# Two bottleneck blocks on one core: the moments of one group of the 3x3 convolution a combination earlier, and smaller transfers at the very end

## The chip, the cores and the metric

The kernel runs on one core of a Trainium2 chip. The metric is device time in microseconds (us) of one execution, from the median of several. TensorE (PE) multiplies matrices, VectorE (DVE), ScalarE (ACT) and GpSimd (POOL) work on elements, and SyncE (SP) issues most of the transfers between the chip's memory (SBUF) and device memory.

## The reference

Two residual bottleneck blocks follow each other, each on 64 images of 1024 channels and 14x14 points, all in float32:

```python
out = relu(bn(conv(x, w1, b1, 1, 0), g1, be1))      # 1x1, 1024 -> 256 channels
out = relu(bn(conv(out, w2, b2, 1, 1), g2, be2))    # 3x3, 256 -> 256
out = bn(conv(out, w3, b3, 1, 0), g3, be3)          # 1x1, 256 -> 1024
x   = relu(x + softplus(residual_scale)[0] * out)
```

`bn` takes mean and variance of each channel over all 64 images and all points of this very batch. So no value can be normalised before its convolution is done for the whole batch, and each convolution ends with a point at which everything waits for the last statistics.

## The kernel before, in words

The activations between the convolutions (`y_all`, 128 partitions x 2 x 12544 float32) stay in SBUF. Images lie in pairs (`T` = 32 tiles of two) and, for the 3x3 convolution, in `NG` = 8 groups of `GI` = 8 images.

`conv2` (L549) is the 3x3 convolution, as a Winograd scheme over rows: each group is made of six combinations (`NF` = 6, three pairs in the order 1 and 2, 3 and 4, 5 and 0). For each combination, `combine` (L583) builds a sum of rows `r` on VectorE (L639 to L665), `sums` of its halves on VectorE (L596), `diffs` on GpSimd (L599), and loads the transformed filters on SP (L618). `Products` (L668) then multiplies on PE into PSUM banks `m`, `l`, `even` and `odd`. ScalarE copies `m` into `even` and `odd` as a start value (L697, L699) and copies `l` out into `ls` (L699). `finish` (L764) is a coroutine that takes the six combinations of a group one after the other and makes output rows out of them: in its tiles `a` (tag `fa`) and `d` (`fb`) it collects partial sums; rows 1 and 2 of every four are written at L795 and L796, row 3 and the end row at L810 and L811, and row 0 with the last combination `cb`. In the text a combination's place in its group is `k`, from 0 to 5.

Row 0 is `a` plus the columns of `cb`, where the columns are the PSUM bank plus or minus `ls`. In groups 0 to 6, VectorE writes bank and `ls` into `y` (L833, four instructions of 128x224) and two accumulating transfers on GpSimd's queue (L838) add `a` to it. In the last group (7) VectorE first adds `ls` into `a` (`cb.add`, L752, two instructions of 128x448) and then adds bank and `a` into `y` (L831), without a transfer.

The statistics of the 3x3 convolution come from two sources. For groups 0 to 6, and rows 1 and 2 of group 7, ScalarE passes over the rows with an accumulating activation (`moment`, L857: identity and square, for each of the two slots `o`), into the throw-away tile `idle`. For the rest of group 7 VectorE takes statistics (`stat`, L771, at L774). `merge` (L860) sums the moments up (a reduction on VectorE at L865 for each slot, the rest on GpSimd) into an entry beside those statistics. Then `aggregate` (L1168) and `affine` (L1184 to L1209) make scale and shift.

`long_work` (L890) says at which combination ScalarE does which long piece: the normalisation of the next group, or a moment of the group before. For the last group there is no next group, so its table differs. The order in which items go through the engines is the loop of L910 to L925; a scheduler then places the instructions on each engine where no order is written out, so that an edit may move neighbours.

After conv2 comes the Gram stage (`gram`, L935): the rows are normalised (ScalarE L539, VectorE L951), transposed (on PE at L981 for the first seven pieces, by transfers through `home` or `ws` and VectorE L993 for the rest) and multiplied with themselves on PE, which gives the statistics of the last convolution beforehand. Then the last convolution runs, in block 0 mixed with the first convolution of block 1.

In block 1 the last convolution is `final` (L1091): pairs of tiles, and at the end tile 31 alone with `residual` (L1074). It makes eight channel slots `o` one after the other: two matmuls, an addition with scale on VectorE (L1082), a ReLU on ScalarE (L1083); after every second slot SP issues a transfer of two slots to `out` (L1086).

Of the kernel before, what the change touches and what calls it, by code (L numbers as in the profile page):

```python
# [45 lines left out]
CS = C // P  # L46
MS = M // P
G = 2
T = N // G
# [16 lines left out]
NG = N // GI  # L66
# [25 lines left out]
def bottlenecks(ctx: ExitStack, tc: tile.TileContext, x, w1s, w2s, w3s, pars, out):  # L92
    nc = tc.nc
# [455 lines left out]
    def conv2(psum, pool, b, par, aff, affine_of, stats):  # L549
# [22 lines left out]
        def new(tag, tiles=RT):  # L572
            v = pool.tile([P, MS * RT * LINE], FP, tag=tag, name=tag, bufs=BUFS.get(tag, 1))
            return v[:, : MS * tiles * LINE].rearrange("p (s r l) -> p s r l", s=MS, r=tiles)
# [5 lines left out]
        def stt(to, a, by, c):  # L580
            return nc.vector.scalar_tensor_tensor(to, a, by, c, ALU.mult, ALU.add)
# [172 lines left out]
        def half(f, q):  # L754

            return f.rearrange("p o r (i q c) -> p q (o r i) c", i=GI, q=2)[:, q]

        def outputs(c):
            f = new("f", c.lines // GI)
            for q in c.banks:  # L760
                c.add(q, half(f, q), c.column(q))
            return f

        def finish():  # L764


            for g in range(NG):
                out_rows = [y_grp[:, :, g, k::4, :] for k in range(4)]
                last_group = g == NG - 1

                def stat(k, lines):  # L771
                    if last_group:
                        for o in range(MS):
                            nc.vector.bn_stats(stats[:, o, 1 + k, :], lines[o])  # L774

                ca = yield
                fa = None if ca.ls is None else outputs(ca)
                fb = outputs((yield))
                a, d = new("fa"), new("fb")
                if fa is not None:  # L780
                    nc.vector.tensor_add(a, fa, fb)
                    nc.vector.tensor_sub(d, fa, fb)
                else:
                    for q in ca.banks:
                        nc.vector.tensor_tensor(half(a, q), ca.column(q), half(fb, q), ALU.add)
                        nc.vector.tensor_tensor(half(d, q), ca.column(q), half(fb, q), ALU.subtract)

                fa = outputs((yield))
                fb = outputs((yield))
                c, e = new("fc", full), fa  # L790
                nc.vector.tensor_add(c, fa, fb)
                nc.vector.tensor_sub(e, fa, fb)
                a3, d3 = (v[:, :, :full] for v in (a, d))
                for o in range(MS):
                    stt(out_rows[1][:, o, :full], e[:, o], 2.0, d3[:, o])  # L795
                    stt(out_rows[2][:, o], c[:, o], 4.0, a3[:, o])  # L796
                nc.vector.tensor_add(a3, a3, c)
                stt(d3, e, 8.0, d3)
                if g == 0:
                    begin(out_rows[1][:, :, :full])  # L800
                if last_group:
                    for o in range(MS):
                        lines = y_grp[:, o, g, 1 : 1 + 4 * full].rearrange("p (r k) l -> p r k l", k=4)[:, :, :2]
                        for k in range(2):
                            moment(lines, idle[:, : 2 * full * LINE].rearrange("p (r k l) -> p r k l", k=2, l=LINE), o, k, g)

                fa = outputs((yield))

                end = y_grp[:, :, g, H - 1]
                nc.vector.tensor_add(out_rows[3], d3, fa[:, :, :full])  # L810
                nc.vector.tensor_add(end, d[:, :, full], fa[:, :, full])  # L811
                stat(0, [out_rows[3][:, o] for o in range(MS)])
                stat(1, [end[:, o] for o in range(MS)])
                if last_group:
                    merge()

                cb = yield
                if last_group:
                    for q in cb.banks:
                        cb.add(q, half(a, q), half(a, q))  # L820

                for j, q in enumerate(cb.banks):
                    for o in range(MS):
                        to, more = (
                            v[:, o].rearrange("p r (i q c) -> p q r i c", i=GI, q=2)[:, q] for v in (out_rows[0], a)
                        )
                        bank, ls = (
                            v[:, o].rearrange("p (r i c) -> p r i c", r=RT, c=WH) for v in (cb.banks[q], cb.ls)
                        )
                        if last_group:  # L830
                            nc.vector.tensor_add(to, bank, more)  # L831
                        else:
                            nc.vector.tensor_tensor(to, bank, ls, ALU.add if q == EVEN else cb.op)  # L833
                    stat(2 + j, [out_rows[0][:, o].rearrange("p r (i q c) -> p q r i c", i=GI, q=2)[:, q] for o in range(MS)])
                if not last_group:

                    for o in range(MS):
                        nc.gpsimd.dma_start(out=out_rows[0][:, o], in_=a[:, o], accum_op=ALU.add)  # L838
            yield
# [8 lines left out]
        def begin(lines):  # L848

            mv = small.tile([P, MS, nc.vector.BN_AGGR_DIM], FP, tag="mv_first", name="mv_first")  # L850
            for o in range(MS):
                nc.vector.bn_stats(first_stats[:, o], lines[:, o])
            for o in range(MS):
                nc.vector.bn_aggr(mv[:, o, :], first_stats[:, o])
            nc.vector.tensor_scalar(center, mv[:, :, 0], -1.0, None, ALU.mult)

        def moment(y, to, o, k, g):  # L857
            act(to, y, (AF.Identity, AF.Square)[k], bias=center[:, o : o + 1], accum_out=moments[:, o, k, g : g + 1])

        def merge():  # L860

            n = GPX * (NG - 1) + 2 * full * LINE
            m = small.tile([P, MS, 2], FP, tag="m12", name="m12")
            for o in range(MS):
                nc.vector.tensor_reduce(m[:, o], moments[:, o], mybir.AxisListType.X, ALU.add)  # L865
            eng = nc.gpsimd
            eng.tensor_scalar(m, m, 1.0 / n, None, ALU.mult)
            var = small.tile([P, MS], FP, tag="m12var", name="m12var")
            eng.tensor_tensor(var, m[:, :, 0], m[:, :, 0], ALU.mult)
            eng.tensor_sub(var, m[:, :, 1], var)  # L870
            eng.tensor_sub(m[:, :, 0], m[:, :, 0], center)

            for half in range(2):
                to = stats[:, :, 0, 3 * half : 3 * half + 3]
                eng.memset(to[:, :, 0], n / 2)
                eng.tensor_copy(to[:, :, 1], m[:, :, 0])
                eng.tensor_scalar(to[:, :, 2], var, n / 2, None, ALU.mult)
# [12 lines left out]
        def long_work(g, k):  # L890

            i = ("norm 0", "norm 1", 0, 1, 2, 3)[k] if g else (None, "norm 0", "norm 1", None, None, None)[k]
            if g + 1 == NG:
                i = (None, 0, 1, 2, 3, None)[k]
            if i in ("norm 0", "norm 1"):
                s = int(i[-1])
                norm(s, y_grp[:, s, g + 1], aff, act)
            elif i is not None:  # L900
                o = i // 2
                moment(y_all[:, o, (g - 1) * GPX : g * GPX], idle, o, i % 2, g - 1)

        made, finished = items(), finish()
        next(finished)
        queue = [next(made) for i in range(3)]
        queue[0].start()
        for k in range(NG * NF):  # L910
# [14 lines left out]
            queue = queue[1:] + list(itertools.islice(made, 1))  # L925
# [148 lines left out]
    def residual(psum, xt, b, t, w3, aff, made=()):  # L1074

        scale, shift = aff
        to = mids[t] if b == 0 else out[t]
        step = 2 if b == 1 and t == T - 1 else CS
        for o in range(CS):
            ps = made[o] if o < len(made) else conv3(psum, t, o, w3)  # L1080
            v = xt[:, o, :]
            nc.vector.scalar_tensor_tensor(v, ps, scale[:, o : o + 1], v, ALU.mult, ALU.add)  # L1082
            nc.scalar.activation(v, v, AF.Relu, bias=shift[:, o : o + 1])  # L1083
            if (o + 1) % step == 0:
                queue = nc.gpsimd if step == CS else nc.sync
                queue.dma_start(  # L1086
                    out=to[:, (o + 1 - step) * PX : (o + 1) * PX],
                    in_=xt[:, o + 1 - step : o + 1, :].rearrange("p s f -> p (s f)"),
                )
# [294 lines left out]
```

## Time and profile before

| | |
|---|---|
| median of 4 runs | 1990.44 us (1990.05 to 1991.28) |
| the profiled execution: its time, its span | 1992.06 us, 1990.3 us |
| granted PE clock, mean | 0.991 of full speed |
| first conv2: last matmul ends, first of the Gram stage starts | 597.14 us, 603.32 us |
| second conv2: the same | 1581.66 us, 1587.83 us |
| last matmul of all ends | 1985.34 us |

The profile is of one execution with its start at 0. A line of a timeline gives start in us, duration in us, engine, source line, operation, output `<-` inputs with their shapes, a count, and in brackets how long the engine had been idle and what released it. Rows that follow each other without a break on one engine overlap by some 0.08 us, since the next starts while the last drains. A line of windows gives a stretch, its length, each engine's busy time in it with the number of instructions, then the granted PE clock, the busy share of the DMA engines and GB/s.

### The profile page before, as it was taken

Reading aid. Unit: us, or ns where it says so; the run is one execution under the profiler, and the core shown is the slowest. Engines: PE = TensorE matmul, PEld = TensorE weight load, DVE = VectorE, ACT = ScalarE, POOL = GpSimd, SP = SyncE. Lnnn points to the kernel's source line nnn. Section 1 sums busy time; section 2 is a strip of 40 time slices with the busy share of each in tenths; the row PEclk is TensorE's granted clock in tenths of the full one; section 3 lists DMA queues with packets and bytes.
Section 4 is the critical chain, followed back from the end, with each engine's and each line's share of the span. In section 5 each row is a group of like instructions: output and inputs, shape, how many; then the busy total and the mean of one; then the engine's idle time right before and its main releaser. Section 6 shows DMA issues by size and latency. Waiting matters only on the chain.

```text
span 1990.3 us, 27740 instructions
## 1 busy us (share of the span) xinstructions
PE 1943.4 (98%) x9560; PEld 1638.4 (82%) x9560; DVE 1572.6 (79%) x2844; ACT 955.5 (48%) x1947; POOL 690.7 (35%) x738
## 2 busy tenths in 40 slices
PE   9999999999998999999999999999999899999998
PEld 5555558999997889999999999989999887555554
DVE  5788758999888567776776777699999874899997
ACT  2222214556565055555555555445556541555555
POOL 0111101333325133333333333223242260766665
PEclk9999999999999999999999999999999998999999
DMA  7876725676757534444444444266777485699998
GB/s 276 291 252 244 256 97 183 171 208 202 203 157 203 192 130 163 188 169 170 186 163 174 183 162 182 85 202 192 210 197 207 131 206 203 242 340 333 342 335 293
DMA packets 191341, 414.09 MB, mean 208 GB/s; under 512 B 27296, under 2 KB 159040, under 8 KB 174688
## 3 DMA queue, kind: packets, MB, share of 16 engines
q1 hardware_dynamic: 161728, 329.06, 48.3%
q0 software_dynamic: 24000, 32.39, 7.1%
q10 hardware_dynamic: 5472, 50.86, 6.1%
q8 instruction: 76, 1.25, 0.3%
q14 instruction: 65, 0.53, 0.1%
HBM read 267.95 MB, written 115.87 MB: 193 GB/s over the span
## 4 chain that ended last, share of the span: by engine, by line
PE 80%; DVE 13%; DMA 4%; ACT 2%; issue 1%; POOL 0%; DVEq 0%; SPq 0%; ACTq 0%
PE ay L172 17%; PE cy L172 13%; PE cp L172 11%; PE ap L172 10%; PE even L172 6%; PE odd L172 6%; PE ax L172 5%; PE m L172 5%; PE l L172 4%; PE cx L172 4%; DMA x<-mid 2%; DVE x L456 2%; DMA out<-x 1%; PE ps L172 1%; DVE sums L596 1%
## 5 line engine op out<-in xcount | busy, mean ns | idle before, releaser
L330 ACT ACTIVATE cu<-cy,scale 128x196 f32<-128x196 f32 (+1 forms) x552 | 256.8, 474 | 297.6 <-PE cy L172 290.3
L599 POOL TENSOR_TENSOR diffs<-r 128x448 f32<-128x448 f32 (+1 forms) x80 | 139.1, 1756 | 328.5 <-DVE r L643 150.0
L330 ACT ACTIVATE x<-x,shift 128x392 f32<-128x392 f32 x368 | 211.7, 614 | 68.8 <-POOL x L482 52.8
L456 DVE SCALAR_TENSOR_TENSOR x<-cp,scale,x 128x196 f32<-128x196 f32 (+1 forms) x368 | 178.1, 484 | 83.0 <-PE cp L172 81.0
L477 POOL TENSOR_TENSOR x<-x,cu 128x196 f32<-128x196 f32 (+1 forms) x184 | 167.5, 910 | 170.9 <-ACT cu L330 170.5
L172 PE MATMUL cy<-ct,ws 128*128 128x196 f32 (+1 forms) x736 | 221.7, 383 | 2.5 <-ACT cu L330 2.5
L172 PE MATMUL ay<-at,ws 128*128 128x196 f32 (+1 forms) x752 | 209.3, 381 | 1.0 <-ACT au L330 1.0
L482 POOL TENSOR_TENSOR x<-x,cu 128x392 f32<-128x392 f32 x124 | 125.9, 1015 | 190.7 <-DVE x L456 185.9
L172 PEld LDWEIGHTS ay<-at,ws 128*128 128x128 f32 x752 | 136.3, 190 | 35.1 <-ACT au L330 1.9
L172 PEld LDWEIGHTS cy<-ct,ws 128*128 128x128 f32 x736 | 133.6, 190 | 36.9 <-ACT cu L330 3.8
L503 POOL TENSOR_TENSOR x<-x,cu 128x392 f32<-128x392 f32 x120 | 125.0, 1042 | 83.6 <-DVE x L456 75.7
L172 PE MATMUL m<-sums,ua 128*128 128x224 f32 (+1 forms) x752 | 145.5, 336 | 0.0
L172 PEld LDWEIGHTS m<-sums,ua 128*128 128x128 f32 x752 | 131.4, 189 | 0.2
L456 DVE SCALAR_TENSOR_TENSOR x<-cx,scale,x 128x196 f32<-128x196 f32 (+1 forms) x184 | 89.2, 485 | 50.8 <-PE cx L172 50.5
L172 PE MATMUL cy<-y,w 128*128 128x196 f32 (+1 forms) x404 | 126.6, 400 | 0.0
L172 PE MATMUL even<-v,ub 128*128 128x224 f32 (+1 forms) x640 | 123.8, 334 | 1.6 <-ACT even L699 1.6
L172 PE MATMUL cx<-y,w 128*128 128x196 f32 (+1 forms) x404 | 125.3, 396 | 0.0
L172 PE MATMUL odd<-v,ub 128*128 128x224 f32 (+1 forms) x640 | 123.8, 335 | 0.1
L172 PE MATMUL l<-diffs,ub 128*128 128x224 f32 (+1 forms) x640 | 122.0, 333 | 0.0
L172 PE MATMUL cp<-zt 128*128 128x257 f32 x392 | 119.8, 387 | 1.9 <-DVE zt L987 1.7
L330 ACT ACTIVATE au<-ay 128x196 f32<-128x196 f32 (+1 forms) x141 | 53.6, 380 | 140.3 <-PE ay L172 139.6
L172 PE MATMUL cp<-y,ws 128*128 128x196 f32 (+1 forms) x368 | 113.7, 391 | 3.7 <-DVE x L456 2.3
(217 smaller groups left out, 4392.3 us busy)
## 6 DMA issues: line engine op xcount, KB each, us to landing
x<-in_x SPq DMA_DIRECT2D x62, 1568.0 KB, 6.8
ub<-u SPq DMA_DIRECT2D x80, 768.0 KB, 4.8
x<-mid SPq DMA_DIRECT2D x32, 1568.0 KB, 10.2
mid<-x ACTq DMA_DIRECT2D x31, 1568.0 KB, 5.1
out<-x SPq DMA_DIRECT2D x124, 392.0 KB, 7.0
ua<-u SPq DMA_DIRECT2D x94, 256.0 KB, 3.0
ub<-u SPq DMA_DIRECT2D x14, 1024.0 KB, 5.9
u<-y POOLq DMA_DIRECT2D x40, 256.0 KB, 6.3
```

The lines of the kernel that those rows point to most:

```text
L172: tc.keep_in_program_order(nc.tensor.matmul(*args, **kw))
L330: tc.keep_in_program_order(nc.scalar.activation(*args, **kw))
L456: nc.vector.scalar_tensor_tensor(v, bank, self.scale[:, o : o + 1], v, ALU.mult, ALU.add)
L477: nc.gpsimd.tensor_add(self.part(1, 1), self.part(1, 1), u3)
L482: nc.gpsimd.tensor_add(v, v, self.u12)
L503: nc.gpsimd.tensor_add(v, v, self.u12[:, i * self.n : (i + 1) * self.n])
L596: nc.vector.tensor_add(sums, r[:, :, :, WH:], r[:, :, :, :WH])
L599: nc.gpsimd.tensor_sub(diffs, r[:, :, :, :WH], r[:, :, :, WH:])
```

## The change

In `finish`, group 6 is completed the way the last group was: `ls` is added into `a`, then bank and `a` into `y`, both on VectorE; the two accumulating transfers of that group go. In `long_work`, the four moments of group 6 move from `k` = 1 to 4 of the last group to `k` = 0 to 3. In `residual`, the last tile of all goes out in five transfers in place of four: slots 0 and 1, 2 and 3, 4 and 5, then 6 alone, all on SP, then 7 alone on ScalarE's queue.

```diff
@@ finish
+                by_transfer = g < NG - 2
...
                 cb = yield
-                if last_group:
+                if not by_transfer:
                     for q in cb.banks:
                         cb.add(q, half(a, q), half(a, q))
...
-                        if last_group:
+                        if not by_transfer:
                             nc.vector.tensor_add(to, bank, more)
                         else:
                             nc.vector.tensor_tensor(to, bank, ls, ALU.add if q == EVEN else cb.op)
...
-                if not last_group:
+                if by_transfer:
 
                     for o in range(MS):
                         nc.gpsimd.dma_start(out=out_rows[0][:, o], in_=a[:, o], accum_op=ALU.add)
@@ long_work
             if g + 1 == NG:
-                i = (None, 0, 1, 2, 3, None)[k]
+                i = (0, 1, 2, 3, None, None)[k]
@@ residual
-        step = 2 if b == 1 and t == T - 1 else CS
+        tail = b == 1 and t == T - 1
         for o in range(CS):
...
+            step = CS if not tail else 1 if o + 2 >= CS else 2
             if (o + 1) % step == 0:
-                queue = nc.gpsimd if step == CS else nc.sync
+                queue = nc.gpsimd if step == CS else nc.scalar if o + 1 == CS else nc.sync
```

## The prediction

> **What bounds the kernel now.** I read the page first (shares, then the chain that ended last), then the timelines of the two places that the change touches, engine by engine, and at the end the windows with granted clock and DMA share.
>
> ```profile
> PE 1943.4 (98%) x9560; PEld 1638.4 (82%) x9560; DVE 1572.6 (79%) x2844; ACT 955.5 (48%) x1947; POOL 690.7 (35%) x738
> PE 80%; DVE 13%; DMA 4%; ACT 2%; issue 1%; POOL 0%; DVEq 0%; SPq 0%; ACTq 0%
> ```
>
> TensorE is busy 98% of the span and is 80% of the chain. So the change can only pay where PE stands still: at the end of each 3x3 convolution (conv2, one per block, PE idle 597.14 to 603.32 us and 1581.66 to 1587.83) and behind the last matmul (1985.34 to 1990.3). This is the end of the first conv2, in order of time (start, duration, engine, line):
>
> ```profile
> 594.09 0.19 ACT L330 ACTIVATION_READ_ACCUMULATOR idle<-y,center 128x1 f32 x1
> 594.30 1.60 ACT L330 ACTIVATE idle<-y,center 128x1568 bf16<-128x1568 f32 x1
> 594.35 1.26 DVE L774 BATCH_NORM_STATS2 stats<-y 128x6 f32<-128x336 f32 x4
> 595.45 1.69 PE L172 MATMUL odd<-v,ub 128*128 128x224 f32 x8
> 595.81 0.19 ACT L330 ACTIVATION_READ_ACCUMULATOR idle<-y,center 128x1 f32 x1
> 595.90 0.52 ACT L699 ACTIVATE ls<-l 128x448 f32<-128x448 f32 x1
> 596.03 0.17 DVE L865 TENSOR_REDUCE m<-moments 128x2 f32<-128x16 f32 x1 [0.42 <-ACT idle L330]
> 596.46 1.16 DVE L752 TENSOR_TENSOR fa<-fa,ls 128x448 f32<-128x448 f32 x2 [0.26 <-ACT ls L699]
> 597.54 0.68 DVE L831 TENSOR_TENSOR y<-even,fa 128x224 f32<-128x224 f32 x2
> ```
>
> See that the 1568-wide moment at 594.30 is the last long piece on ScalarE, that the copy `ls` queues behind it, and that VectorE waits twice, 0.42 us for the moment and 0.26 us for `ls`. From 596.46 on the chain stays on VectorE (with one square root on ScalarE) through the affine to the first normalised rows, and PE waits for those.
>
> Next, the boundary between group 6 and group 7, where work is added: VectorE, then ScalarE.
>
> ```profile
> 561.57 0.84 DVE L581 SCALAR_TENSOR_TENSOR r<-t 128x672 f32<-128x672 f32 x1
> 566.01 0.68 DVE L833 TENSOR_TENSOR y<-odd,ls 128x224 f32<-128x224 f32 x2
> 571.58 0.49 DVE L581 SCALAR_TENSOR_TENSOR r<-y,r 128x336 f32<-128x336 f32 x1
> 574.37 0.62 DVE L752 TENSOR_TENSOR f<-even,ls 128x448 f32<-128x448 f32 x1 [2.30 <-PE even L172]
> ```
> ```profile
> 568.84 0.53 ACT L699 ACTIVATE odd<-m 128x448 f32<-128x448 f32 x1
> 572.77 0.54 ACT L699 ACTIVATE ls<-l 128x448 f32<-128x448 f32 x1 [3.40 <-PE l L172]
> ```
>
> Both engines have a hole just there: VectorE 2.30 us, ScalarE 3.40 us, both ended by PE. PE itself shows no idle time from 534 to 597.
>
> **Part 1, group 6 completed by VectorE.** Per conv2 it removes two accumulating transfers (L838; 1.27 to 1.84 us each of GpSimd, 4.1 to 7.5 us from issue to landing) and adds two in-place additions `fa<-fa,ls` 128x448. These exist already in the last group: the row above gives 1.16 us for two, 1.08 us from the first's start to what follows. The four row writes keep their form (L833 becomes L831: medians 378 and 378 to 382 ns). The program order of the changed kernel on VectorE is: `fa` even, L810, L811, `fa` odd, the first `r`, even rows, `sums`, odd rows, `v`, the second `r`, and so on. With the steps from start to start in this trace (0.53 for 448 elements, 0.77 for L810, 0.30 for L811, 0.77 for `r`, 0.60 for a pair of rows, 0.42 for `sums`), the first `r` starts at 563.70, 2.13 us later than 561.57; even rows at 564.47 (564.50 before) and odd rows at 565.49 (566.01 before), so the PSUM banks come free no later. `sums` of that `r` is 1.7 us late, done near 565.6; PE reads it at 574.10. GpSimd's `diffs` from it is some 2 us late (done near 565.4 before); PE reads it at 576.77. Behind the added work, VectorE's hole shrinks from 2.30 to about 1.2 us. All of it is covered; with the cover gone it would cost 1.08 us a block, or 2.13 us through the first `r`.
>
> GpSimd's queue gets two transfers shorter, but its next row (`diffs`, 570.88) waits for VectorE's `r` anyway: nothing gained. SP's loads in conv2 are not moved.
>
> **Part 2, moments one combination earlier.** The four 1568-wide moments (1.60 + 0.19 us, about 1.7 us in the queue) move from 578.03, 581.07, 586.23 and 594.30 to 569.27, 578.03, 581.07 and 586.23. Three slots held one already. The new first one runs 569.27 to 570.97 in the 3.40 us hole, 1.8 us ahead of `ls` at 572.77; it needs the odd rows, done near 566.1. Without the accumulating transfer it waits for no landing. The queue behind it is `ls`, which VectorE reads at 574.37, so 1.8 us of lateness is free.
>
> What goes is the moment at 594.30. `ls` starts there instead of at 595.90. But VectorE is busy with four statistics rows until 595.55 (1.26 us, less the usual overlap). Then: reduction 595.55, first addition 595.68 (0.13 us later, as at 592.48 to 592.61), against 596.46. Gain **0.78 us**, not the 1.60 us that ScalarE is freed: VectorE's own queue is late next. Behind that stand PE (its last matmul ends at 597.14, VectorE reaches the odd rows at 597.95, 0.81 us to spare) and GpSimd's merge (starts 0.48 us earlier, ends 598.27, read at 599.13). The second conv2 has the same rows: 1580.97 against 1580.19, 0.78 us. Together 1.56 us.
>
> **Does the next stage keep it?** After each hole the Gram stage starts at half the clock.
>
> ```profile
> 597.00:603.00 6.00, 0.15 (x1) 0.00 (x0) 5.56 (x25) 1.27 (x3) 1.74 (x13) 0.96 0.40 127
> 603.00:609.00 6.00, 5.47 (x21) 4.73 (x22) 4.34 (x7) 6.00 (x6) 0.39 (x1) 0.50 0.62 224
> ```
>
> The third number from the right is the granted clock: 0.50 for the first 6.0 us of work in block 0; in block 1 finer windows show it for 4.5 us. The PE restart after `zt` at 619.23 comes 22.09 us after conv2's last matmul, the same event in block 1 (1603.17) after 21.51. So 1.5 us less of half clock was worth 0.58 us, 0.39 us per us. If the clock returns at the same moment though work starts 0.78 us earlier, 0.31 us of the 0.78 is lost. If the clock never falls in the shorter hole, 4.5 to 6.0 us of half clock go, at that rate up to 2.3 us more. Value taken: 0.78 per stage, bounds 0.47 and 3.1.
>
> [...]
>
> **Part 3, the last transfers.** The last tile left in four transfers of 392 KB; now in three of these and two of 196 KB, the last from ScalarE's queue.
>
> ```profile
> 1986.02 0.62 ACT L1083 ACTIVATE x<-x,shift 128x392 f32<-128x392 f32 x1 [0.69 <-DVE x L1082]
> 1986.67 0.33 SPq L1086 DMA_DIRECT2D out<-x  x1
> ```
> ```profile
> 1987.50:1988.00 0.50, 0.00 (x0) 0.00 (x0) 0.00 (x0) 0.00 (x0) 0.00 (x0) 1.00 1.05 414
> 1988.00:1988.50 0.50, 0.00 (x0) 0.00 (x0) 0.00 (x0) 0.00 (x0) 0.00 (x0) 0.80 0.95 376
> ```
>
> The issue follows the activation by 0.03 us; the data move for 1.0 us; 2.3 us from issue to landing. Half the bytes take half of the 1.0: gain **0.5 us**. The other 196 KB leave a matmul group earlier (activation done 1985.32) into DMA engines that are nearly idle from 1986.0 to 1987.5. ScalarE's issue costs the same (L491: 0.33 us, 0.03 us behind its activation). Bounds: nothing (if the rest of the 2.3 us is all that counts) to 0.6.
>
> **Sum.** 0.78 + 0.78 + 0.5 = 2.06 us. The profiled execution took 1992.06 us (span 1990.3 and 1.8 around it): 1990.0. The median of the other runs is 1990.44, 1.62 lower; I take the same 2.06 off it: **1988.4 us**. That is 0.10%; about 0.2% (4.0 us) is what a measurement of this kernel tells from no change.
>
> **Rivals.**
> *The clock does more.* For it: the hole shrinks, and the two stages already differ by 0.58 us. One stage that escapes adds up to 2.3 us: 1988.4 to 1986.1. Chance 0.18, 0.06 of it below 1986.46.
> *The gain is swallowed.* ScalarE's chain of normalisations (26.11 us without a break) and the transfers of `home` (a 4.00 us wait at 1608.05 in block 1) could set the Gram stage's pace. Against it: both start from the affine that moves earlier. Clock loss in both stages and no gain at the tail: 1.56 - 0.62 = 0.94, so 1989.5; all swallowed, 1990.4. Chance 0.15.
> *Slower: the later `r` reaches PE.* At the boundary `r`, `sums` and GpSimd's `diffs` come later, and GpSimd is slowed beside a busy VectorE (562.56: 2.81 us, 566.23: 0.93 us, one shape). Price if nothing covered it: 2.13 + 1.88 = 4.0 us a block, 8.0 less 2.06: 1996.4. It decides where `diffs` is later by 11 us (565.4 to 576.77) or `sums` by 10 (563.9 to 574.10); the steps above give about 2. Chance 0.07, half of it beyond 0.2%.
> *Forecast:* chance 0.60, its own range 1987.8 (tail 0.6, half a microsecond of clock) to 1989.3 (0.47 in each stage, 0.2 at the tail).
>
> Range: 1986.2 to 1990.4. Faster by over 0.2%: 0.07 (0.06 of the first rival, 0.01 of the forecast); slower: 0.04 (half of the third rival); within: 0.89.
>
> **What would show it.** Right: no 1568-wide moment behind 590 us, the first `fa<-fa,ls` of the last group 0.8 us nearer to PE's last matmul (0.7 before it to 1.5 before it), PE's hole 5.4 us, the last transfer landing 1.8 us after issue. Wrong: PE idle between groups 6 and 7, `ls` at 572.77 late, or a Gram stage whose restart after the hole does not come earlier.

## The result

| | before | after |
|---|---|---|
| median | 1990.77 us (60 runs, 1988.92 to 1993.44) | 1988.90 us (42 runs, 1986.71 to 1990.71) |
| the profiled execution: its time, its span | 1992.06 us, 1990.3 us | 1989.31 us, 1987.5 us |

The ratio is 0.9990, 95% interval 0.9986 to 0.9995: 1.87 us or 0.1% faster (1.0 to 2.8 us by the interval), where 2.06 us was forecast. Of the 0.5 us between the forecast 1988.4 and 1988.90, 0.33 are the start: the median of before is 1990.77 over 60 runs, not 1990.44. The profiled executions differ by 2.75 us.

**The page after.** TensorE is as busy as before, and it is still 80% of the chain.

```profile
PE 1942.9 (98%) x9560; PEld 1638.3 (82%) x9560; DVE 1575.1 (79%) x2848; ACT 957.0 (48%) x1947; POOL 683.2 (34%) x734
```

**The end of the first conv2 after**, all engines in order of time (start, duration, engine, line, operation):

```profile
594.45 0.52 ACT L699 ACTIVATE ls<-l 128x448 f32<-128x448 f32 x1
594.61 1.27 DVE L776 BATCH_NORM_STATS2 stats<-y 128x6 f32<-128x336 f32 x4
595.72 1.69 PE L172 MATMUL odd<-v,ub 128*128 128x224 f32 x8
595.79 0.15 DVE L867 TENSOR_REDUCE m<-moments 128x2 f32<-128x16 f32 x1
595.86 1.15 DVE L752 TENSOR_TENSOR fa<-fa,ls 128x448 f32<-128x448 f32 x2
...
602.62 1.08 PE L983 MATMUL cy<-ident,y 128*128 128x128 f32 x4 [5.20 <-issue]
```

The 1568-wide moment is gone from here, and so are both waits of VectorE: its four rows now follow each other without a break, from the statistics through the reduction to the additions. The first `fa<-fa,ls` stands 1.55 us ahead of PE's last end (597.41) where it stood 0.69 us ahead before. PE's hole is 5.20 us (6.17 before), in block 1 5.56 (6.17).

**The boundary between groups 6 and 7 after**: VectorE, then ScalarE.

```profile
561.84 0.61 DVE L752 TENSOR_TENSOR fa<-fa,ls 128x448 f32<-128x448 f32 x1
...
563.98 0.85 DVE L581 SCALAR_TENSOR_TENSOR r<-t 128x672 f32<-128x672 f32 x1
...
565.35 0.92 DVE L596 TENSOR_TENSOR sums<-r 128x336 f32<-128x336 f32 x1
...
574.63 0.63 DVE L752 TENSOR_TENSOR f<-even,ls 128x448 f32<-128x448 f32 x1 [0.63 <-PE even L172]
```
```profile
569.63 1.60 ACT L330 ACTIVATE idle<-y,center 128x1568 bf16<-128x1568 f32 x1
...
573.03 0.55 ACT L699 ACTIVATE ls<-l 128x448 f32<-128x448 f32 x1 [1.71 <-PE l L172]
```

The added work and the moved moment fit into the two holes: VectorE's is 0.63 us now (2.30 before), ScalarE's 1.71 (3.40), and both are still ended by PE. PE has no idle time here.

**The end of the program after**: the last issue, and the view of DMA issues (KB each, us from issue to landing).

```profile
1984.41 0.34 ACTq L1090 DMA_DIRECT2D out<-x  x1
```
```profile
out<-x ACTq DMA_DIRECT2D x1, 196.0 KB, 1.9
```

From the activation's end (1984.38) to the end of the span are 3.15 us, 3.64 before.

**Where the 2.75 us lie.** The two profiles, cut at the same events, with the time of half granted clock inside each stage (from the clock records of the trace):

| stage | after minus before | half clock before, after |
|---|---|---|
| first hole (conv2's end to first transposition) | -0.97 | |
| first Gram stage | -0.97 | 6.83, 6.83 (hole included) |
| last convolution of block 0 with the first two of block 1 | +1.64 | 6.83, 10.24 |
| second hole | -0.62 | |
| second Gram stage | +0.37 | 6.83, 6.83 (hole included) |
| last convolution of block 1 | -1.98 | 10.24, 6.83 |
| behind the last activation | -0.50 | |

(The 0.27 us that are left lie mostly ahead of the first conv2.) A Gram stage is counted here from its first transposition to the first matmul of the last convolution's statistics. Holes and tail give 2.09 us, close to the forecast 2.06. The other stages, which the change does not touch, add and take up to 2 us: the two long ones where the half clock got longer or shorter by 3.41 us, the Gram stages where the same 6.83 us lay differently against the hole. Up to the last matmul, half clock comes only in whole multiples of 3.41 us in these two traces (3.41, 6.83, 10.24). That 3.41 us more or less of it goes with 1.6 and 2.0 us here accounts for the part of the 2.75 us that the change did not make, and would account for much of the spread of the runs (4.5 us before, 4.0 after).

### The profile page after: what moved, and what is told of

It is laid out like the page before. It is cut to its first block, busy times and chain, and to the rows that moved or that the text cites. A ratio compares the mean times of both kernels' runs of the same rounds, so it can differ in the third digit from the quotient of the medians.

```text
span 1987.5 us, 27738 instructions
## 1 busy us (share of the span) xinstructions
PE 1942.9 (98%) x9560; PEld 1638.3 (82%) x9560; DVE 1575.1 (79%) x2848; ACT 957.0 (48%) x1947; POOL 683.2 (34%) x734
## 4 chain that ended last, share of the span: by engine, by line
PE 80%; DVE 13%; DMA 3%; issue 1%; ACT 1%; SPq 0%; POOL 0%; DVEq 0%; ACTq 0%
PE ay L172 17%; PE cy L172 13%; PE cp L172 11%; PE ap L172 10%; PE even L172 6%; PE odd L172 6%; PE ax L172 5%; PE m L172 5%; PE cx L172 4%; PE l L172 4%; DMA x<-mid 2%; DVE x L456 2%; PE ps L172 1%; DVE sums L596 1%; DVE f L752 1%
```

## The experiments

Each kernel was made from the kernel before or after; holes and stages are read at the same events as in the table above. Every hole and stage is read from one profiled execution of its kernel; where a kernel's time rests on a single execution too, that is said.

### Each half of the group's change alone

My theory: the moment can move a combination earlier only because the accumulating transfer is gone, for it would wait for that transfer's landing. The rival: the queue of ScalarE has slack there and the additions bring nothing.

`moments_alone`, from before:
```diff
-                i = (None, 0, 1, 2, 3, None)[k]
+                i = (0, 1, 2, 3, None, None)[k]
```


> The moments are moved as in the change, but group 6 is still completed by the accumulating transfers. My theory (the additions on VectorE are there to let the moments start): the first moment stands in ScalarE's queue ahead of the copy ls and must wait for the landing, which comes 4.1 to 7.5 us after an issue at 567 to 569.7 us, so it starts near 575 instead of 569.6 and ls near 577 instead of 573. VectorE's read of ls and the start value of the next even bank come 2 to 4 us late, and PE stands 1 to 3 us between groups 6 and 7 in each block. The hole behind conv2 is 5.2 to 5.6 us as in the changed kernel. Time: 1990.77 - 1.6 + (2 to 6), so 1991 to 1995. Rival (the queue has enough slack to take the wait): PE shows no idle time there, and the time is that of the change without its tail, 1989.4.

Measured: 1989.2 us, ratio 0.9988 (0.9979 to 0.9997); holes 5.29 us in both blocks, 0.88 less. ScalarE at the boundary, then VectorE:

```profile
571.82 1.60 ACT L330 ACTIVATE idle<-y,center 128x1568 bf16<-128x1568 f32 x1 [2.15 <-DMA y<-fa]
...
573.42 0.52 ACT L699 ACTIVATE ls<-l 128x448 f32<-128x448 f32 x1
```
```profile
574.67 0.62 DVE L752 TENSOR_TENSOR f<-even,ls 128x448 f32<-128x448 f32 x1 [2.30 <-PE even L172]
```

The moment does wait 2.15 us for the landing, as my theory had it, and `ls` comes 0.4 us later than after the whole change. But the reader of `ls` starts at 574.67 with or without that, because it waits for PE. My theory falls: the wait is real and costs nothing.

`adds_alone`, from after:
```diff
-                i = (0, 1, 2, 3, None, None)[k]
+                i = (None, 0, 1, 2, 3, None)[k]
```
and the old tail.

> Group 6 is completed by VectorE, the moments stay where they were, the tail is that of before. Theory (the two extra additions a block lie in VectorE's 2.30 us hole, and by themselves they bring nothing): hole behind conv2 6.17 us as before, no idle time on PE between groups 6 and 7, time within 0.5 us of before but for the clock's phase, 1990 to 1991. Rival (the transfers removed were in the way, or the additions cost 1.08 us a block): 2 us either way.

Measured: 1991.55 us, ratio 1.0001 (0.9992 to 1.0010); holes 6.07 and 6.42 us (6.17 and 6.17 before), VectorE's hole at the boundary 0.65 us, no idle time of PE. So the additions are covered, as predicted, and bring nothing in conv2: the hole is 0.10 us shorter in block 0 and 0.25 longer in block 1. Both appear here without the moments: see `ones_early`.

`groups_alone` is the changed kernel with the old tail.

> The change without its tail. Theory: holes behind conv2 of 5.2 and 5.6 us as in the changed kernel (6.17 before), 3.66 us from the last ReLU to the end of the span as before (3.15 in the changed kernel), time 0.5 us above the changed kernel, 1989.4. Rival (the holes' gain is eaten in the Gram stage): holes as said, but time that of before, 1990.8.

Measured: 1990.2 us, ratio 0.9994 (0.9985 to 1.0003); holes 5.20 and 5.55 us, tail 3.64. The holes are those of the whole change and the tail is that of before, so the parts add up in the profiles. The medians of these three (1989.2, 1991.55, 1990.2) can't rank them more finely than the windows of half clock allow, and by its time alone `groups_alone` can't be told from before; the holes can be told apart.

### What is late next in the hole

`no_row_stats`, one execution, from after: the statistics of row 3 and of the end row of the last group are left out, and their entries filled by GpSimd.
```diff
-                stat(0, [out_rows[3][:, o] for o in range(MS)])
-                stat(1, [end[:, o] for o in range(MS)])
+                if last_group:
+                    nc.gpsimd.memset(stats[:, :, 1:3, :], 1.0)
```


> The changed kernel without the four statistics of row 3 and the end row on VectorE in the last group (0.30 us each, 1.2 us in its queue; their place in the statistics is filled with ones, so this part of the variance is left out). Theory (after the change VectorE's own queue sets the end of conv2, and PE's last matmul comes 0.8 us behind it): the hole gets shorter by 0.8 to 1.0 us, to 4.3 in block 0 and 4.7 in block 1, and the odd rows then wait for PE. Rival (the long moment's end or GpSimd's merge sets the end): the hole stays at 5.2 and 5.6 us.

Measured: holes 4.54 and 4.55 us. VectorE at the first one:

```profile
594.70 1.16 DVE L752 TENSOR_TENSOR fa<-fa,ls 128x448 f32<-128x448 f32 x2 [0.22 <-ACT ls L699]
```

With the four rows gone (1.27 us together) the hole shrinks by 0.66 us in block 0, a little less than the 0.8 expected, and by 1.01 in block 1, where the two aggregates also stand closer (0.32 us, 0.67 after the change; see `ones_early`). So VectorE's queue was what bound the hole after the change, as the prediction put it, and behind it come `ls` (0.22 us of waiting) and then PE itself: the odd rows start at 597.15, PE's last matmul ends at 597.12.

`ones_early`, from after: the memset of `ones` moves from the statistics of the last convolution (L1053) to the start of the program, in a tile that stays.

> The changed kernel with the column of ones of the Gram statistics made once at the start, not by a memset between the two aggregations of each conv2, where the memset waits for eight transfers one after the other. Theory (these waits are why the holes of the changed kernel are 5.2 us in block 0 and 5.6 us in block 1 where both were 6.17): 0.24 us less in block 0, 0.6 us less in block 1, both holes 4.9 to 5.1 us. The waits move to the first copy of zt, behind PE. Rival (the wait was hidden behind the aggregation): no hole changes by more than 0.1 us. Time 0.5 to 1.0 us below the changed kernel, 1988.2, in the noise of the clock.

Measured: 1988.7 us, ratio 0.9990 (0.9981 to 1.0000); holes 5.01 and 5.02 us. This is block 1 after the change, where the memset stands between the two aggregates:

```profile
1583.52 0.27 DVE L1172 BATCH_NORM_AGGREGATE mv<-stats 128x2 f32<-128x30 f32 x1
1584.19 0.06 DVE L1053 MEMSET ones<- 128x1 f32 x1 [0.40 <-issue]
1584.19 0.29 DVE L1172 BATCH_NORM_AGGREGATE mv<-stats 128x2 f32<-128x30 f32 x1
```

The two aggregates start 0.67 us apart (0.41 before the change). Without the memset the pair takes 0.42 us for both, and the blocks are equal: 0.18 us of the first hole and 0.54 us of the second were the memset's. It writes a reused tile, and four instructions of its line that wait for semaphores stand ahead of it in VectorE's queue; which of them holds it for the 0.40 us the profile does not show.

### The tail

`tail_sp`: the changed kernel, the last transfer on SP instead of ScalarE's queue. `tail_fine`: the last slot cut once more, 98 KB on each queue. One execution each.
```diff
-                queue = nc.gpsimd if step == CS else nc.scalar if o + 1 == CS else nc.sync
+                queue = nc.gpsimd if step == CS else nc.sync
```


> The changed kernel with all five last transfers on SP. Theory (the halved size made the gain at the tail, not the other queue): 3.15 us from the last ReLU to the end of the span, as in the changed kernel. Rival (ScalarE's queue made a part of it): 3.3 to 3.66 us.

> The changed kernel with the last 196 KB in two halves of 98 KB, one on ScalarE's queue and one on SP's, issued at the same time. Theory (what counts is the bytes that are left when the last ReLU ends, and these do not change: both halves share the same 16 engines): no gain, 3.1 to 3.2 us from the last ReLU to the end. Rival (the time goes by the size of one transfer): 0.25 us less, 2.9 us.

Measured, from the last activation's end to the end of the span: 3.64 us before, 3.15 after, 3.13 for `tail_sp`, 3.23 for `tail_fine`. So the other queue made no difference here (0.02 us), and cutting the last 196 KB into two transfers issued together brought nothing: the 98 KB took 1.8 and 2.0 us to land, the 196 KB 1.9 and the 392 KB 2.3. The gain of 0.5 us is that of the first halving alone. It left fewer bytes behind the last activation, as the prediction priced it; `tail_fine` left as many, so whether still fewer would gain more is not shown.

### The half clock

`warm`, from after: six matmuls 128x448 without a reader behind conv2's last matmul.
```diff
+        for _ in range(6):
+            matmul(psum.tile(n, "m"), ident, ident[:, :1].to_broadcast([P, n]), start=True, stop=True)
```


> The changed kernel with six matmuls that nobody reads (ident times a broadcast column, 448 wide, 0.75 us each) on PE behind the last matmul of each conv2, so that PE is idle for less than 1 us there instead of 5.2 to 5.6. They end some 0.7 us before the first rows are ready. Theory (the granted clock falls in these holes and half clock costs the Gram stage about 0.4 us per us): no half clock at the start of either Gram stage, and each is 1.0 to 2.3 us shorter; time 1985.5 to 1987.5 against 1988.9. Rival (the chain of normalisations on ScalarE sets the pace there, the clock does not): full clock but the same start of the vector transposes within 0.3 us, time 1988.5 to 1989.2.

Measured: 1987.0 us, ratio 0.9979 (0.9970 to 0.9988). The holes end when they ended without the dummies (in block 0 the first transposition starts at 603.89 us, after the change at 602.62, with conv2 1.28 us earlier there), the clock is full at the start of both Gram stages (1.00 from 601.5 to 612 us in block 0), and these stages are shorter than before the change by 1.07 and 0.94 us (by 0.97 less and 0.37 more in the profile after). But one stretch of half clock in each block (6.83 us in `warm`, up to 10.24 in the other traces so far) stays behind the Gram stage, where PE never stands still. This is `before` there, windows and then PE's timeline.

```profile
687.00:691.00 4.00, 4.00 (x21) 3.68 (x21) 0.96 (x6) 0.02 (x1) 0.00 (x0) 0.60 0.00 0
691.00:695.00 4.00, 4.00 (x8) 1.96 (x7) 3.86 (x19) 1.27 (x3) 0.00 (x0) 0.54 0.00 0
```
```profile
683.61 3.63 PE L172 MATMUL ax<-g,w 128*128 128x1 f32 x32
687.10 2.90 PE L172 MATMUL ax<-ones,q 128*128 128x1 f32 x16
```

PE is busy for all of the 8 us, and the clock is halved from 687.8 to 694.6. What runs from 683.6 are the matmuls of the last convolution's statistics, `conv3_stats`, with one column each (128x1): 24 in the kernel, 48 in the trace, where each stands as two records with a weight load of its own, one every 0.109 us. The expectations count the 48 records. Three kernels test whether it is these, `both_wide`, `both_dense` and later `both_64`, on a base, `both`, that has the dummies and the early memset.

> The changed kernel with the six dummy matmuls behind each conv2 and the memset of `ones` moved to the program's start, so that the two small edits stand together and make the base of the next two kernels. If they add up: holes of 5.0 us in both blocks (against 5.20 and 5.56), no half clock at the start of the Gram stages, and a median some 0.7 us under that of the dummies alone: about 1986.3. If the memset's 0.4 us is only an effect of how the trace draws it, 1987.0 as with the dummies alone.

Measured: 1987.16 us, ratio 0.9975 (0.9967 to 0.9984); holes 5.01 and 5.02 us, no half clock at the Gram stages, 6.83 us of it in each `conv3_stats`. The holes and the clock add up. Whether the time does, the runs can't say: the ratio is 0.0004 under that of `warm`, and each interval is wider. In the profiles it does not: against `warm` the holes of `both` are 0.19 and 0.53 us shorter, and its Gram stages 0.17 and 0.72 us longer. In block 1 VectorE starts the pieces from `home` at 1609.97 (1608.83 in `warm`), held by their transfers, and PE waits for it, as it does not in `warm`:

```profile
1609.97 2.49 DVE L998 STREAM_TRANSPOSE zt<-home 128x512 f32<-128x512 f32 x4 [3.69 <-DMA home<-y]
...
1610.74 0.70 PE L172 MATMUL cp<-zt 128*128 128x257 f32 x2 [0.46 <-DVE zt L998]
```

So a shorter hole is not kept everywhere: at full clock the transfers of `home`, named in the prediction's rival of the swallowed gain, are late next in block 1 of `both` (3.69 us of VectorE's waiting, 0.46 of PE's).

`both_wide`: the narrow matmuls 32 columns wide, one of the columns read.
```diff
-                matmul(quad[:, o, 0:1], w3[:, s, o, :], means[s], ...)
+                matmul(quad[:, o, 0], w3[:, s, o, :], means[s].to_broadcast([P, WD]), ...)
```


> The same kernel with the 48 matmuls 128x1 of the last convolution's statistics made 128x32 (the vector repeated by a broadcast, one column of 32 read), number and weight loads unchanged: they are spaced 0.109 us at full clock by their weight loads, so the wider ones should take no longer. In that place PE stands never still, but the clock halves there in every profile so far, for 6.8 or 10.2 us in each block. If the throttle counts work in the array, and so many narrow matmuls look idle to it, the wider ones keep the clock: the half clock there goes, 3.4 to 5.1 us a block, a median near 1979. If 32 columns are still too few, or if the throttle looks at something else, the half clock stays as it is and the median is that of the narrow kernel, about 1986.3.

Measured: 1985.97 us, ratio 0.9972 (0.9961 to 0.9982). The spacing stays 0.109 us. In the profile `conv3_stats` has its 6.83 us of half clock still in block 0 and none in block 1: neither of the two outcomes written down, but one between them.

`both_dense`: the narrow matmuls, with three dummies 128x512 between them in each block.

> The kernel of the dummies and the early memset with three more dummy matmuls 128x512 in each block between the 128x1 matmuls of the last convolution's statistics (after 16, after 32 and after 40 of 48), 0.43 us each or 2.6 us in all. If the clock halves there because a whole window of 3.41 us is without dense work, three pieces of at most 1.8 us hold no such window: the half clock goes (6.8 to 10.2 us of it a block, half of it lost), 6.8 to 10.2 us less 2.6: a median of 1976 to 1982. If the half clock there has another cause, the median is 2.6 us later than the kernel without them: about 1989.

Measured: 1993.99 us (1986.00 to 1996.41), ratio 1.0009 (0.9999 to 1.0019): 6.8 us slower than `both`, and the half clock grew to 13.65 and 10.24 us. I had the dummy at 0.43 us, which is one record; each is two records, 0.86 us at full clock, so the six cost 5.2 us there and not 2.6. That explains most of the loss, but not the longer half clock: the idea that a piece of dense work inside each window keeps the clock did not hold here.

**A count.** Half clock starts on a fixed grid of 3.413 us in each trace (before the change at 353.32, 602.49, 687.82, 1585.53 and 1670.86 us). For each window of the grid I added up the columns of all its matmuls (0.83 ns a column, from 512 columns in 0.43 us; twice that at half clock, where 392 columns took 0.65 us and not 0.33) and asked what the clock was in the window behind it. From 320 to 1985 us of the 14 traces (that of the last kernel below among them) there are 6,813 windows (from 10 to 320 us the clock is full in all, and no window is filled to less than 0.51):

| window, and the one behind it | number | share of the window filled with columns |
|---|---|---|
| full, then half | 60 | 0.00 to 0.369 |
| full, then full | 6,648 | 0.368 to 0.99 |
| half, then half | 52 | 0.01 to 0.76 of half-clock columns (0.38 of full) |
| half, then full | 53 | 0.79 and more (0.40 of full) |

In these traces one value near 0.37 to 0.39 of what a window can take at full clock divides all but two neighbours (0.368 and 0.369). It is a count over this case's windows; what sets the clock, they do not show. Each case agrees with it: narrow matmuls fill 0.008 of a window; 32 columns 0.24, and it is left to the grid's phase whether denser neighbours lift a window above that value (0.301 in block 0, 0.376 and 0.426 in block 1 of `both_wide`); in `both_dense` the window at 683.1 holds a whole dummy and still only 0.255, and the windows behind it, at half clock, 0.50 to 0.58, where up to 0.76 was followed by half clock again. It also agrees with the holes, none of which kept the clock. A window stays below the value with 2.0 to 2.2 us of idleness in it, so by this estimate a hole over about twice that, 4.0 to 4.3 us, would have half clock behind it in every phase; all 18 holes of 4.54 to 6.42 us in these traces did. Nor need a hole be as long as a window: near 351 us, where no edit reaches, PE has a hole of 1.98 us, and in nine of the 14 traces a window of half clock follows it, in five none: the grid leaves the emptiest window there filled to 0.33 to 0.37 in the nine and to 0.40 to 0.45 in the five.

`both_64` tests the count: 64 columns fill 0.49.
```diff
-                matmul(quad[:, o, 0:1], w3[:, s, o, :], means[s], ...)
+                matmul(quad[:, o : o + WD], w3[:, s, o, :], means[s].to_broadcast([P, WD]), ...)
...
-            matmul(quad[:, o, 1:2], q[:, 0, o * P : (o + 1) * P], ones, ...)
+            matmul(quad[:, CS + o : CS + o + WD], q[:, 0, o * P : (o + 1) * P], ones.to_broadcast([P, WD]), ...)
```


> The kernel of the dummies and the early memset once more, its 48 matmuls 128x1 of the last convolution's statistics made 128x64 (the vector repeated, neighbours overlapping by 63 columns, one column of each left standing), number and weight loads unchanged. A count over the traces so far speaks for a threshold: on a grid of 3.413 us, a stretch in which TensorE takes in columns for less than 0.37 of its full-clock time is followed by one at half clock, and one with more is not. 32 columns every 0.109 us are 0.24 of that, 64 are 0.49. If this count is the cause, the half clock (6.8 us in each block of the base) is gone from both places, whatever the grid's phase, and with it 3.4 us a block: a median of 1980.3 against 1987.2 for 128x1 and 1986.0 for 128x32. If the throttle looks at something else (the weight loads, the time without transfers), the half clock stays and the median with it, 1986 to 1987. If 64 columns are slower than their weight loads, the 48 pieces take longer than 0.109 us each, and 96 x 0.05, some 5 us, is given back.

Measured: **1980.61 us** (1980.12 to 1981.37), ratio 0.9948 (0.9935 to 0.9962). The windows of the same place, and then PE's timeline there:

```profile
687.00:691.00 4.00, 2.57 (x8) 1.17 (x7) 3.86 (x23) 0.41 (x2) 0.00 (x0) 1.00 0.00 0
691.00:695.00 4.00, 4.00 (x12) 2.36 (x13) 3.52 (x6) 3.04 (x6) 0.00 (x0) 1.00 0.00 0
```
```profile
681.42 3.68 PE L172 MATMUL ax<-g,w 128*128 128x64 f32 x32
684.93 1.95 PE L172 MATMUL ax<-ones,q 128*128 128x64 f32 x16
686.72 1.54 PE L172 MATMUL cx<-y,w 128*128 128x392 f32 x4
688.09 1.48 PE L172 MATMUL cy<-y,w 128*128 128x392 f32 x4
691.00 1.23 PE L172 MATMUL ay<-y,w 128*128 128x392 f32 x3 [1.43 <-DVE x L1086]
```

The clock is full throughout there, the wider matmuls take no longer (3.51 us from the first of 32 to the first of the next 16, that is 0.110 each), and the five runs spread over 1.3 us where ten of `warm` spread over 6.5 and eleven of `both` over 5.1. In the profile of `both_64` one window of half clock is left, near 353 us. PE now waits 1.43 us at 689.57, since VectorE's scale and shift are the late ones once PE is fast: that is a part of why block 0 gives only 1.7 us against `both`. Block 1 gives 4.3; why that is more than the 3.4 us of its half clock I did not trace. The medians differ by 6.5 us, where 6.9 was expected, but they were taken beside different runs of before (1991.57 us for `both`, 1990.45 for `both_64`); by the ratios it is 5.4 us.

## Why the prediction was right

*VectorE's own queue late next, 0.78 us and not 1.60.* Right in mechanism, shown by the unbroken rows after the change and by `no_row_stats`. Against PE's last matmul the first addition moved 0.86 us; it follows the reduction by 0.07 us and not by 0.13. The holes moved 0.97 and 0.62, together 1.59 where 1.56 was forecast. That the sum fits so closely is in part luck: what is over and above the 0.86 is the two aggregates and the memset between them, 0.10 us better in block 0 and some 0.25 us worse in block 1 (`adds_alone` has both without the moments, `moments_alone` has 0.88 in both blocks, and without the memset both holes are equal).

*The additions are covered.* Right, with less to spare than forecast. In this profile conv2 starts 0.25 us later than in that of before; with that taken off, the first `r` stands at 563.73 (563.70 forecast), the even rows at 564.50 (564.47) and the odd rows at 565.93 (565.49; 566.01 before), so the banks come free no later. VectorE's hole is 0.63 us and not 1.2, because `sums` got slower there (336 elements took 0.92 and 1.23 us). The rival "the later `r` reaches PE" did not come: PE has no idle time there in any kernel with the additions. What the rival says of GpSimd shows in two `diffs` of 128x448 before: 2.22 us from 570.88, with VectorE busy for 1.19 of them, and 1.16 us from 573.07, with VectorE idle. Its own pair, 2.81 and 0.93 us, stood beside a VectorE without a break both times, so the 1.88 us in its price is not shown.

*"Without the accumulating transfer it waits for no landing."* True, but beside the point: `moments_alone` waits for the landing and loses nothing. The gain of conv2 came from one line of a table, and the additions were not needed for it.

*The next stage keeps it.* Right where the clock is alike: `groups_alone` has 6.3 us of half clock behind its first hole, `before` 6.0, and the stage lasts 80.29 us in both, with a hole 0.97 us shorter. Between the profiles before and after, the clock's phase decided more. In block 0 the half clock began 2.0 us after conv2's end and not 5.3, so 3.7 us of it lay behind the hole and not 6.0, and the stage was 0.97 us shorter; in block 1 it was 5.5 and not 4.5, and 0.37 longer. That is 0.41 and 0.37 us for each us of half clock, close to the 0.39 of the prediction. But the 0.39 was read at one event near 619 us; over the whole stage the two blocks of `before` differ by 0.13 us and not by 0.58, so the agreement owes something to luck.

*The upper bound of 3.1 us per stage* is mis-sized. It carries the 0.39 over all the half clock, up to 2.3 us for a stage that escapes. `warm` has none, and its stages are only 1.07 and 0.94 us shorter than before: the last 3.7 us of half clock that block 0 still has after the change cost 0.09 us (79.32 against 79.23). The rival "the clock does more" rests on the same price, and no hole of 4.5 us or more (18 of them) escaped the half clock. The grid of 3.413 us is in every trace here, at a place of its own (the first half clock starts at 353.32 us before and 353.68 after); the full-clock windows ahead of half clock were filled with columns to 0.369 at most, those in `conv3_stats` with PE busy all the time.

*The tail, 0.5 us.* Right: 3.64 to 3.15 us, landing 1.9 us after issue (1.8 forecast).

*"The gain is swallowed."* The medians show nothing swallowed (1.87 of 2.06), but their interval of 1.0 to 2.8 us would not show a loss of some tenths; in single runs half clock moves more than the change does. With the clock held full, `both` shows the rival's mechanism, with its `home` transfers.

## What to carry to other kernels

When a long piece moves out of an engine's queue, ask what is late next, and price the gain by that: here 0.8 us of the 1.6 that were freed. Look whether a wait that a change removes had ended before anyone needed it; half of this change removed one that had. And look at the granted clock where PE is busy: the matmuls of one column went with 6.83 us of half clock in each block of `both`, beside their own 0.109 us each, and 63 more columns that nobody reads, at 0.110 us, were the cheapest gain (5.4 to 6.5 us here, against 2 for the change).

## What the runs showed of the hardware that was not expected

- In the 14 traces TensorE's granted clock halved behind 60 full-clock windows of 3.413 us, filled with columns to 0.00 to 0.369, and stayed full behind 6,648 filled to 0.368 to 0.99. Among the 60 are windows with PE idle (0.00), with matmuls of 1 column back to back (0.008) and with some of 32 columns (0.301). It came back behind 53 half-clock windows filled to 0.40 of full and more, and not behind 52 filled to 0.38 at most.
- A matmul of 64 columns took no longer than one of 1 column, each with its own weight load (0.110 us in `both_64`, 0.109 before).
- Much of the run-to-run spread of this kernel goes with the half clock: 1980.12 to 1981.37 us in five runs without it at the four places (two behind the holes, two in `conv3_stats`), 1988.92 to 1993.44 in 60 with it. In `both_dense` the eleven runs go from 1986.00 us at a mean granted clock of 0.999 to 1996.41 at 0.994.
- Before a memset of 0.06 us on a reused tile VectorE stood 0.40 us with no releaser in the profile (block 1 after the change); holes were 0.18 and 0.54 us shorter without it.
- The last transfer landed 2.3, 1.9 and 1.8 to 2.0 us after its issue at 392, 196 and 98 KB.
